# A deformable convolution and a selective scan on one core: state inputs of the last image from a block-diagonal matrix product, a moved split of the corner weighting, and ordered table loads

## The chip, the core and the metric

The kernel runs on one core of a Trainium2 chip. The core has five engines with queues of their own: TensorE (PE; its weight loads are PEld in the profile), VectorE (DVE), ScalarE (ACT), GpSimd (POOL) and SyncE (SP, which here only issues DMAs). Each engine takes its instructions strictly in the order of its queue, and waits at the head of the queue until the semaphores of that instruction are there. The metric is the time of one execution on the device in microseconds. A difference of 0.2% or less cannot be told from no change for this kernel.

## What is computed

The input is four images of 128 x 128 pixels with 128 channels, fp32. Two layers follow each other, each on a normalized copy of its input and added to it. Layer 0 is a deformable 3x3 convolution in two groups of 64 channels: an ordinary convolution gives an offset for each pixel and tap, each tap is then read at a fractional place, as a weighted sum of the four pixels around it (the "corners"), and a depthwise 3x3 and a pointwise convolution follow. Layer 1 is a two-deep stack of Mamba blocks over sequences; the kernel handles each image row of 128 pixels as a sequence of 128 steps for 256 inner channels and 16 states:

```python
out = wa[..., None]*gather(y0i, x0i) + wb[..., None]*gather(y1i, x0i) \
    + wc[..., None]*gather(y0i, x1i) + wd[..., None]*gather(y1i, x1i)
...
deltaA  = jnp.exp(jnp.einsum('btd,dn->btdn', delta, A))
deltaBu = jnp.einsum('btd,btn->btdn', delta * u, Bm)
...
def step(h, xs):
    dA, dBu, c = xs
    h = dA * h + dBu
    y = jnp.einsum('bdn,bn->bd', h, c)
    return (h, y)
```

Here `u` is a SiLU of a short convolution, `delta` a softplus of a small product, and `Bm`, `Cm` (B and C) come from the same product. The result is `(y + u * D) * silu(res)`, multiplied by an output matrix.

## The kernel before

**Stages.** Image 0's statistics and gather table come first. Then layer 0 of image 0 runs alone (`layer0`), together with the tables of the other images. Then a loop over the images lays layer 0 of image b+1 beside layer 1 of image b; for the last image only layer 1 is left. The pace is fixed in program order: for every step of the scan layer so many steps of the gather layer are issued.

**The framework orders the queues.** The kernel text gives a program order. A scheduler places the instructions in each engine's queue when the kernel is built, and may move an independent instruction forward; it keeps every dependency between tiles. `keep_in_program_order` and manual dependencies restrict it further. What it decides is fixed before the kernel runs.

**Layer 0.** Work goes in units: one of nine pairs of taps for four image rows, 288 units per image. `gather` issues eight indirect DMAs for a unit (POOL writes their descriptors), into tiles `gt` of two rows each. `sample` multiplies the gathered corners by their weights `wt` into `gw`: for the first half (h=0) as one VectorE instruction of 1024 elements (L387), for the second half (h=1) as 16 small ScalarE activations with a per-partition scale (L382). TensorE then transposes and adds the corners (L128) and multiplies by the combined convolution weights (L420).

**Layer 1.** A block is four image rows (`TB` = 512 steps); 32 blocks make an image. A job is one block and one of the two Mamba layers, 256 jobs in all; blocks go in pairs, so that the jobs run (0, layer 0), (1, layer 0), (0, layer 1), (1, layer 1). `pre` computes what a job needs: `u` (L530, L540), the gate `g` (L545, L550), the small product `dbl` (L554, L557), and `delta` and `du` = delta times u (L576 to L591). `main` runs the states, two at a time, in eight rounds q: it loads the rows of B and C broadcast over the partitions, takes the exponentials into one of three tiles `da` (L627), forms `hs` = du times B (L661), scans (L667), multiplies by C (L670), and transposes and adds into `y` in PSUM (L128). After the eighth round come the gate (L677), a transposition (L682) and the output product (L687, or L694 and L696). While `main` of a job runs, `pre` of the next one is issued one portion a round: the portion with u and g comes after round q=0.

**The last image** differs: du is turned once per job by TensorE (`turn_du`), so that time lies on the partitions and B is a per-partition scalar. POOL (L646) and ScalarE (L644) make `xs`, TensorE turns it back (L651), and VectorE scans 512 steps at a time straight from PSUM (L653), then multiplies by C (L656).

**Tables.** ScalarE holds one set of function tables at a time. Silu is in another set than Exp and Ln; where the queue changes from one to the other the compiler puts an ACT_TABLE_LOAD, which the profile shows under the line of the instruction that needed it.

Of the kernel before, what the change touches and what calls it, by code (L numbers as in the profile page):

```python
# [17 lines left out]
P = 128  # L18
G = 2
CG = 64  # L20
# [11 lines left out]
XP = DTR + 1 + 2 * NS  # L32

# [30 lines left out]
def block_kernel(ctx: ExitStack, tc: tile.TileContext, a: dict, out: bass.AP):  # L64
# [26 lines left out]
    pb = ctx.enter_context(tc.tile_pool(name="l0b", bufs=1))  # L91
    ps = ctx.enter_context(tc.tile_pool(name="l0ps", bufs=2, space=PSUM))
    psa = ctx.enter_context(tc.tile_pool(name="l0psa", bufs=2, space=PSUM))
# [11 lines left out]
    offw = loadw("offw", [P, NT, 64])  # L105
# [13 lines left out]
    wc = cw.tile([P, NT, NT, CG], F32, name="wc")  # L119
# [14 lines left out]

    dw = loadw("dw", [P, NT, NT], pool=p2, tag="dbl")
# [35 lines left out]
    xn = cw.tile([P, RB + 2, WP], F32, name="xn")  # L171
# [3 lines left out]
    sbuf_s = [cw.tile([P, 4, WP], F32, name=f"s{i}") for i in range(NSB)]  # L175
# [192 lines left out]
    def sample(b, j, u, gts):  # L368
# [3 lines left out]
        for h in range(2):  # L372
# [4 lines left out]
            if h:  # L377

                for r in range(2):
                    for s in range(4):  # L380
                        for v in range(2):
                            nc.scalar.activation(  # L382
                                gw[:, r, s, v], gts[h][:, v, r, s * CG : (s + 1) * CG], AF.Copy,
                                scale=wt[:, u, r0 + r, s, v : v + 1],
                            )
            else:
                nc.vector.tensor_tensor(  # L387
                    gw.rearrange("p r s v c -> p (r s) v c"),
                    gts[h].rearrange("p v r (s c) -> p (r s) v c", c=CG),
                    wv.unsqueeze(3).to_broadcast([P, 8, 2, CG]),  # L390
                    ALU.mult,
                )
# [100 lines left out]
    duts = []  # L493
    n_dut = [0]

    def turn_du(st, nm):

        if not duts:
            duts.append(p2.tile([P, 2, SR, NC * P], F32, tag="hs", name="duts"))
        n_dut[0] += 1  # L500
        dut = duts[0][:, n_dut[0] % 2]
# [8 lines left out]

    def pre(st, l):

        blk = st["blk"]
        nm = f"{blk}_{l}"
# [24 lines left out]
        for c in range(NC):  # L539
            nc.scalar.activation(u[:, c], pus[c], AF.Silu, bias=cvb[:, l, c : c + 1])  # L540
        g = p2.tile([P, SR, NC * P], F32, tag="g", name=f"g_{nm}", bufs=2)
        for i in range(SR // 2):
            px = ps1.tile([P, 2, NC * P], F32, tag="t", name=f"pr_{nm}_{i}")
            for j in range(2):
                nc.tensor.matmul(  # L545
                    px[:, j], h[:, 2 * i + j, DCONV - 1 :], resw[:, l, :],
                    start=(j == 0), stop=True, skip_group_check=True,
                )

            tc.keep_in_program_order(nc.scalar.activation(g[:, 2 * i : 2 * i + 2], px, AF.Silu))  # L550
# [9 lines left out]
        if in_last(blk):  # L560

            pbt = ps1.tile([P, SR, XP], F32, tag="t", name=f"pbt_{nm}")
            for i in range(SR):
                nc.tensor.transpose(pbt[:, i, :], dbl[:, i * P : (i + 1) * P], ident[0:XP, 0:XP])
# [16 lines left out]
        nc.scalar.activation(e, e, AF.Exp, scale=-1.0)  # L581
        nc.scalar.activation(w1, e, AF.Identity, bias=1.0)
        nc.scalar.activation(du, w1, AF.Ln)
        nc.scalar.activation(w1, w1, AF.Identity, bias=-1.0)
# [3 lines left out]
        nc.vector.tensor_tensor(e, w1, e, ALU.subtract)  # L588
        nc.vector.tensor_tensor(de, de, e, ALU.subtract)
        nc.vector.tensor_tensor(de, de, du, ALU.add)  # L590
        nc.vector.tensor_tensor(du, de, u, ALU.mult)  # L591
        st.update(u=u, g=g, delta=de, du=du, bcd=bcd)
        st.pop("dut", None)
        if in_last(blk) and duts:
            yield
            turn_du(st, nm)

    def main(st, l):
# [11 lines left out]
        if in_last(blk) and "dut" not in st:  # L610
            turn_du(st, nm)
        for q in range(NS // NQ):
            bc = []
            for w in range(in_last(blk), 2):
# [8 lines left out]
            for c in range(NC):  # L623
                dv = st["delta"][:, c].rearrange("p (s t) -> p s t", s=SR)
                for n in range(NQ):
                    s = q * NQ + n
                    nc.scalar.activation(  # L627
                        da[:, c, n, :, 1:], dv[:, :, 1:], AF.Exp, scale=aneg[:, l, c, s : s + 1]
                    )
            dc = da.rearrange("p c n s t -> p c (n s t)")  # L630
            cv = bc[-1].rearrange("p n t -> p (n t)").unsqueeze(1).to_broadcast([P, NC, NQ * TB])
            if in_last(blk):


                for n in range(NQ):
                    s = q * NQ + n

                    xs = (p2 if n else pb).tile(
                        [P, SR, NC * P], F32, tag="bc0" if n else "gw", name=f"xs_{nm}_{s}", bufs=2
                    )  # L640
                    for i in range(SR):
                        bv = st["bt"][:, i, s : s + 1]
                        if n:
                            nc.scalar.activation(xs[:, i], st["dut"][:, i], AF.Copy, scale=bv)  # L644
                        else:
                            nc.gpsimd.tensor_scalar(xs[:, i], st["dut"][:, i], bv, None, ALU.mult)  # L646
                    for c in range(NC):
                        pool, tag = (ps, "t") if n else (psa, "acc")
                        px = pool.tile([P, SR, P], F32, tag=tag, name=f"px_{nm}_{s}_{c}")
                        for i in range(SR):  # L650
                            nc.tensor.transpose(px[:, i, :], xs[:, i, c * P : (c + 1) * P], ident)  # L651
                        dn = da[:, c, n].rearrange("p s t -> p (s t)")
                        nc.vector.tensor_tensor_scan(  # L653
                            dn, dn, px.rearrange("p s t -> p (s t)"), 0.0, ALU.mult, ALU.add
                        )
                nc.vector.tensor_tensor(dc, dc, cv, ALU.mult)  # L656
            else:
# [165 lines left out]
```

## Time and profile before

| quantity | us |
|---|---|
| time, median of 3 runs | 25900.95 |
| lowest and highest run | 25897.37 and 25929.91 |
| span of the profiled execution, first to last instruction | 24903.2 |
| busy in the span: TensorE | 19986.7 |
| busy: VectorE | 20935.3 |
| busy: ScalarE | 16107.7 |
| busy: GpSimd | 17956.4 |

The profile is of one execution of its own, whose time from outside is not listed; its span is 997.75 us below the median of the other runs. In the profile each engine's busy time is the union of its instructions' times. Groups of instructions are listed by line, with the name of the tile written, then those read, the shapes, the count, the busy time and the mean of one in ns; after the bar stands the idle time of the engine just before them, and what ended it. L128 is the line of a helper that serves both layers, so its rows are told apart by tile names (`p` for layer 0, `y` for layer 1). A real fp32 product on TensorE shows as two records for one instruction; a transposition shows as one.

### The profile page before, as it was taken

The numbers are of one execution on the slowest core, as the hardware profiler recorded it, in microseconds if no ns is written. First come the engines' busy times: TensorE is split into PE (matmuls) and PEld (weight loads), VectorE is DVE, ScalarE is ACT, GpSimd is POOL, SyncE is SP. The second block draws the span as 40 slices with busy tenths as digits, with TensorE's granted clock in tenths as the row PEclk, the third lists the DMA queues.
The fourth block names the chain that finished last, engine by engine and source line by source line (L and its number), as shares of the span: only waits on it lengthen the run. The fifth ranks groups of instructions, "written<-read, shape, count | busy, mean of one in ns | idle before, by whom it ended". The sixth has DMA issues, their size and how long they took to land. (4 is left out here: it accounts for less than half of the span.)

```text
span 24903.2 us, 331178 instructions
## 1 busy us (share of the span) xinstructions
PE 19986.7 (80%) x121156; PEld 13946.7 (56%) x121156; DVE 20935.3 (84%) x13018; ACT 16107.7 (65%) x38037; POOL 17956.4 (72%) x11270
## 2 busy tenths in 40 slices
PE   5788788888888878888888878888888877878877
PEld 3555455555555555555555555555555556666666
DVE  2221269999999999999999999999999998888888
ACT  2444466666666666666666666666666667888887
POOL 4777777887887857788887866787887845555555
PEclk8999989999999888999999888999999889999999
DMA  4554544454444444454544444454454442222221
GB/s 136 157 159 130 151 142 157 156 161 158 158 159 156 158 145 153 157 162 157 159 161 155 159 150 151 153 163 158 159 160 157 157 138 67 69 69 71 70 69 68
DMA packets 1530815, 3471.82 MB, mean 139 GB/s; under 512 B 243283, under 2 KB 717651, under 8 KB 1529052
## 3 DMA queue, kind: packets, MB, share of 16 engines
q1 hardware_dynamic: 1086812, 2242.08, 28.0%
q0 software_dynamic: 442368, 1208.55, 15.4%
q8 instruction: 951, 15.58, 0.3%
q14 instruction: 684, 5.60, 0.1%
HBM read 3299.19 MB, written 150.47 MB: 139 GB/s over the span
## 5 line engine op out<-in xcount | busy, mean ns | idle before, releaser
L359 POOL DMA_INDIRECT gt<-table,idx x9216 | 15606.0, 1693 | 4665.8 <-issue 2582.2
L627 ACT ACTIVATE da<-de,aneg 128x508 f32<-128x508 f32 x8192 | 5455.4, 711 | 2609.2 <-PE y L128 2357.7
L667 DVE TENSOR_TENSOR_SCAN da<-da,hs 128x2048 f32<-128x2048 f32 x1536 | 6792.2, 4422 | 120.2 <-ACT da L627 23.8
L128 PE MATMUL y<-ident,da 128*128 128x128 f32 x32768 | 4753.9, 306 | 2176.1 <-DVE da L670 1901.2
L420 PE MATMUL acc<-s,wc 128*64 128x256 f32 (+3 forms) x38400 | 6060.3, 439 | 276.7 <-ACT s L401 269.1
L128 PEld LDWEIGHTS y<-ident,da 128*128 128x128 f32 x32768 | 4247.0, 159 | 2997.4 <-DVE da L670 2050.8
L382 ACT ACTIVATE gw<-gt,wt 128x64 f32<-128x64 f32 x18432 | 4613.2, 337 | 1024.2 <-DMA gt<-table,idx 592.1
L420 PEld LDWEIGHTS acc<-s,wc 128*64 128x64 f32 x38400 | 3200.8, 140 | 2440.1 <-issue 1287.5
L128 PE MATMUL p<-ident,gw 128*128 128x128 f32 x18432 | 2896.6, 305 | 1471.5 <-DVE gw L387 1215.5
L646 POOL TENSOR_SCALAR xs<-duts,bt 128x256 f32<-128x256 f32 x2048 | 2349.7, 1164 | 2249.2 <-ACT duts L508 1185.7
L661 DVE SCALAR_TENSOR_TENSOR hs<-du,ones,bc 128x1024 f32<-128x1024 f32 x3072 | 3828.0, 1281 | 0.0
L670 DVE SCALAR_TENSOR_TENSOR da<-da,ones,bc 128x2048 f32<-128x2048 f32 x1536 | 3609.6, 2350 | 31.8
L128 PEld LDWEIGHTS p<-ident,gw 128*128 128x128 f32 x18432 | 2363.9, 157 | 2272.0 <-DVE gw L387 1150.1
L387 DVE TENSOR_TENSOR gw<-gt,wt 128x1024 f32<-128x1024 f32 x1152 | 1403.7, 1219 | 2357.9 <-DMA gt<-table,idx 1883.7
L653 DVE TENSOR_TENSOR_SCAN da<-da,px 128x512 f32<-128x512 f32 x2048 | 2350.6, 1202 | 509.2 <-PE px L651 509.2
L401 ACT COPY s<-p 128x512 f32<-128x512 f32 x1152 | 669.7, 581 | 2102.5 <-PE p L128 2100.1
L530 PE MATMUL pu<-hp,inc 128*128 128x512 f32 x4096 | 1830.4, 594 | 1.1 <-ACT ot L700 0.8
L651 PE MATMUL px<-ident,xs 128*128 128x128 f32 x8192 | 1213.5, 287 | 537.8 <-DVE da L653 322.1
L651 PEld LDWEIGHTS px<-ident,xs 128*128 128x128 f32 x8192 | 972.2, 147 | 818.0 <-POOL xs L646 329.3
L530 PEld LDWEIGHTS pu<-hp,inc 128*128 128x128 f32 x4096 | 747.8, 190 | 813.1 <-issue 809.3
L656 DVE TENSOR_TENSOR da<-da,bc 128x2048 f32<-128x2048 f32 x512 | 1172.0, 2289 | 6.6
L644 ACT ACTIVATE xs<-duts,bt 128x256 f32<-128x256 f32 x2048 | 894.3, 499 | 19.3 <-PE px L651 18.8
(133 smaller groups left out, 14768.7 us busy)
## 6 DMA issues: line engine op xcount, KB each, us to landing
bc<-bcd SPq DMA_DIRECT2D x3584, 512.0 KB
gt<-table,idx POOLq DMA_INDIRECT x9216
table<-xg SPq DMA_DIRECT2D x1016, 64.0 KB
xt<-in_x SPq DMA_DIRECT2D x124, 320.0 KB
xr<-in_x SPq DMA_DIRECT2D x128, 256.0 KB
x<-xo SPq DMA_DIRECT2D x128, 256.0 KB
x1t<-x SPq DMA_DIRECT2D x128, 256.0 KB
x1t_o<-x SPq DMA_DIRECT2D x128, 256.0 KB
```

Of the source, the lines that this page charges most:

```text
L128: nc.tensor.matmul(o, v, ident, is_transpose=True, start=start, stop=stop, skip_group_check=True)
L359: nc.gpsimd.indirect_dma_start(out=gt[:, v, r], out_offset=None, in_=flat, in_offset=bass.IndirectOffsetOnAxis(ap=idx[:, ri, o : o + 1], a ...
L382: nc.scalar.activation(gw[:, r, s, v], gts[h][:, v, r, s * CG : (s + 1) * CG], AF.Copy, scale=wt[:, u, r0 + r, s, v : v + 1],)
L420: nc.tensor.matmul(accs[b, j + i0][CG * g : CG * g + CG, q : q + rb - ra, :], wc[sl, v, e, :], st[p + 4 * g if p < 4 else 8][sl, ra:rb, kx ...
L530: nc.tensor.matmul(px.rearrange("p (s t) -> p s t", s=SR), inc[:, l, j, c * P : (c + 1) * P], h[:, :, j : j + P], start=(j == 0), stop=(j ...
L627: nc.scalar.activation(da[:, c, n, :, 1:], dv[:, :, 1:], AF.Exp, scale=aneg[:, l, c, s : s + 1])
L646: nc.gpsimd.tensor_scalar(xs[:, i], st["dut"][:, i], bv, None, ALU.mult)
L651: nc.tensor.transpose(px[:, i, :], xs[:, i, c * P : (c + 1) * P], ident)
L653: nc.vector.tensor_tensor_scan(dn, dn, px.rearrange("p s t -> p (s t)"), 0.0, ALU.mult, ALU.add)
L661: nc.vector.scalar_tensor_tensor(hs[:, :, n, :], st["du"], ones[:, 0:1], bc[0][:, n].unsqueeze(1).to_broadcast([P, NC, TB]), op0=ALU.mult, ...
L667: nc.vector.tensor_tensor_scan(df, df, hs.rearrange("p c n t -> p (c n t)"), 0.0, ALU.mult, ALU.add)
L670: nc.vector.scalar_tensor_tensor(dc, dc, ones[:, 0:1], cv, op0=ALU.mult, op1=ALU.mult)
```

## The change

Four things are changed together.

1. **Last image.** Layer 0's memory is released when the last image's first `pre` gets to `du`, and four banks of PSUM and new tiles are opened in its place. delta times u of 32 time steps of each of the four rows is put beside each other, turned as before, and multiplied on TensorE by a matrix `D` that holds B on a diagonal (POOL makes it, from B and a constant mask, for four states at once). The product is written to one PSUM tile `px` for four states of one half of the channels; one scan then takes all 2048 elements. Exponentials run two rounds ahead into four tiles. `main_last` replaces the branch in `main`.
2. **Corner weighting.** For image 0 all of it goes to VectorE. For the other images ScalarE takes both rows of the second half and one of the two rows of the first half; VectorE keeps one row.
3. **Table loads.** A load of the set that holds both exp and ln is placed by hand after the Silus of each `pre`. Dependencies without a semaphore put each Exp and Ln behind the last such load, and the next Silu behind every Exp and Ln issued so far.
4. **Softplus.** The subtraction of 1 (L584 on ScalarE) is folded into the next VectorE instruction.

```diff
+    def exp(i):
+        if tables["exp"] is not None:
+            order(i, tables["exp"])
+        tables["after"].append(i)
+        return i
+
+    def silu(i):
+        if tables["after"]:
+            for j in tables["after"]:
+                order(i, j)
+            tables["after"] = []
+        elif tables["silu"] is not None:
+            order(i, tables["silu"])
+        tables["silu"] = i
+        return i
...
-            nc.scalar.activation(u[:, c], pus[c], AF.Silu, bias=cvb[:, l, c : c + 1])
+            silu(nc.scalar.activation(u[:, c], pus[c], AF.Silu, bias=cvb[:, l, c : c + 1]))
...
-            tc.keep_in_program_order(nc.scalar.activation(g[:, 2 * i : 2 * i + 2], px, AF.Silu))
+            silu(nc.scalar.activation(g[:, 2 * i : 2 * i + 2], px, AF.Silu))
+        tables["exp"] = silu(nc.scalar.preload_act_table_set("natural_log_exp_and_others"))
         yield
...
-        nc.scalar.activation(e, e, AF.Exp, scale=-1.0)
+        exp(nc.scalar.activation(e, e, AF.Exp, scale=-1.0))
         nc.scalar.activation(w1, e, AF.Identity, bias=1.0)
-        nc.scalar.activation(du, w1, AF.Ln)
-        nc.scalar.activation(w1, w1, AF.Identity, bias=-1.0)
+        exp(nc.scalar.activation(du, w1, AF.Ln))
...
-        nc.vector.tensor_tensor(e, w1, e, ALU.subtract)
+        nc.vector.scalar_tensor_tensor(e, w1, -1.0, e, op0=ALU.add, op1=ALU.subtract)
...
-                    nc.scalar.activation(
+                    exp(nc.scalar.activation(
                         da[:, c, n, :, 1:], dv[:, :, 1:], AF.Exp, scale=aneg[:, l, c, s : s + 1]
-                    )
+                    ))
...
+            alone = 2 if b == 0 else 0 if h else 1
+            for r in range(alone, 2):
+                for s in range(4):
+                    for v in range(2):
+                        nc.scalar.activation(
+                            gw[:, r, s, v], gts[h][:, v, r, s * CG : (s + 1) * CG], AF.Copy,
+                            scale=wt[:, u, r0 + r, s, v : v + 1],
+                        )
+            if alone:
                 nc.vector.tensor_tensor(
-                    gw.rearrange("p r s v c -> p (r s) v c"),
-                    gts[h].rearrange("p v r (s c) -> p (r s) v c", c=CG),
-                    wv.unsqueeze(3).to_broadcast([P, 8, 2, CG]),
+                    gw[:, 0:alone].rearrange("p r s v c -> p (r s) v c"),
+                    gts[h][:, :, 0:alone].rearrange("p v r (s c) -> p (r s) v c", c=CG),
+                    wv[:, 0 : 4 * alone].unsqueeze(3).to_broadcast([P, 4 * alone, 2, CG]),
                     ALU.mult,
                 )
...
+    def make_d(st, u):
+        d = le["r"].tile([P, SR, NU, QW], F32, tag="D", name=f"D_{st['nm']}_{u}", bufs=3)
+        nc.gpsimd.tensor_tensor(
+            d, st["bt"][:, :, NU * u : NU * u + NU].unsqueeze(3).to_broadcast([P, SR, NU, QW]),
+            mask.unsqueeze(1).unsqueeze(1).to_broadcast([P, SR, NU, QW]), ALU.mult,
+        )
+        st["D", u] = d
+
+    def fill(st, k):
+        u, c = divmod(k, NC)
+        px = le["ps"].tile([P, SR, NU, P], F32, tag="dbu", name=f"px_{st['nm']}_{k}")
+        for q in range(SR):
+            for g in range(SR):
+                o = slice(g * QW, (g + 1) * QW)
+                nc.tensor.matmul(
+                    px[:, g, :, q * QW : (q + 1) * QW],
+                    st["dut"][o, q, c * P : (c + 1) * P], st["D", u][o, q],
+                    start=True, stop=True, skip_group_check=True,
+                )
+        st["px"] = px
...
+        for k in range(nk):
+            u, c = divmod(k, NC)
+            if c == 0:
+                ct = le["r"].tile([P, NU, TB], F32, tag="ct", name=f"ct_{nm}_{u}", bufs=2)
+                n0 = NS + NU * u
+                nc.sync.dma_start(ct, st["bcd"][n0 : n0 + NU, :].partition_broadcast(P))
+                if k + NC < nk:
+                    make_d(st, u + 1)
+            if k + 2 < nk:
+                exps(st, l, k + 2)
+            elif nst:
+                exps(nst, nl, k + 2 - nk)
+            hs = le["r"].tile([P, SR, NU, P], F32, tag="he", name=f"he_{nm}_{k}", bufs=3)
+            nc.vector.tensor_tensor_scan(
+                hs.rearrange("p s n t -> p (s n t)"),
+                st.pop(("da", k)).rearrange("p s n t -> p (s n t)"),
+                st["px"].rearrange("p s n t -> p (s n t)"), 0.0, ALU.mult, ALU.add,
+            )
+            if k + 1 < nk:
+                fill(st, k + 1)
+            elif nst:
+                fill(nst, 0)
+            nc.vector.tensor_tensor(
+                hs, hs, ct.rearrange("p n (s t) -> p s n t", s=SR), ALU.mult
+            )
+            for s in range(SR):
+                for i in range(NU):
+                    add_transposed(y[:, s, c], hs[:, s, i, :], False, u == NS // NU - 1 and i == NU - 1)
+            yield
```

`exps` issues the exponentials of four states of one half; `SR` = 4 is the number of rows in a block, `QW` = 32, `NU` = 4. The four values of `g` in `fill` are four slices of 32 partitions, and each writes to a PSUM bank of its own.

## Prediction

> **What bounds the kernel now.** I read the row of slices first: it shows stages with different limits.
>
> ```profile
> DVE  2221269999999999999999999999999998888888
> ACT  2444466666666666666666666666666667888887
> POOL 4777777887887857788887866787887845555555
> ```
>
> A slice is 622.6 us. POOL leads in slices 2 to 5 (image 0's gathers alone), DVE is full from slice 7 to 33 (gathers of images 1 to 3 beside the scan layer of images 0 to 2), and falls to eight tenths at the end (the scan layer of image 3 alone). The windows put the borders at the first and last scan of L667 (columns: PE, PEld, DVE, ACT, POOL busy):
>
> ```profile
> 420.00:3340.00 2920.00, 2388.58 (x15078) 1498.61 (x15079) 655.25 (x994) 1308.02 (x4857) 2220.72 (x2223) 0.91 0.50 146
> 3340.00:20570.00 17230.00, 13968.57 (x83567) 9637.80 (x83565) 16351.24 (x8935) 11263.14 (x26734) 13273.45 (x6884) 0.90 0.48 156
> 20570.00:24903.00 4333.00, 3469.45 (x21628) 2706.43 (x21628) 3804.24 (x2876) 3468.27 (x6208) 2349.73 (x2048) 0.93 0.21 69
> ```
>
> I call them A, B, C. B has 192 jobs (one block, one layer): 17230/192 = 89.7 us each, DVE busy 16351/192 = 85.1, so 4.6 idle. C has 64 jobs: 67.5 us (L677, once a job, recurs every 67.5 us), DVE busy 59.4. Why DVE hardly rests in B is in the groups by line of 6000 to 20000 us (156 jobs):
>
> ```profile
> L667 DVE TENSOR_TENSOR_SCAN da<-da,hs 128x2048 f32<-128x2048 f32 x1248 | 5518.6, 4422 | 96.8 <-ACT da L627 20.3 <-DVE hs L661 1.0
> ...
> L387 DVE TENSOR_TENSOR gw<-gt,wt 128x1024 f32<-128x1024 f32 x708 | 860.8, 1216 | 496.6 <-DMA gt<-table,idx 464.5 <-PE p L128 27.2 <-PE y L128 4.7
> ```
>
> The scan waits on its exps for 20.3 us in all, and most DVE idle is the wait for gathers (464.5/156 = 3.0 us a job). That the exps never hold the scan is what the change touches. The timeline of one job's start shows what runs there:
>
> ```profile
> 10000.97 4.42 DVE L667 TENSOR_TENSOR_SCAN da<-da,hs 128x2048 f32<-128x2048 f32 x1
> ...
> 10006.43 2.35 DVE L670 SCALAR_TENSOR_TENSOR da<-da,ones,bc 128x2048 f32<-128x2048 f32 x1
> ...
> 10008.83 1.97 PE L128 MATMUL y<-ident,da 128*128 128x128 f32 x16 [0.61 <-DVE da L670]
> ...
> 10010.63 5.32 PE L530 MATMUL pu<-hp,inc 128*128 128x512 f32 x12
> ...
> 10011.27 4.42 DVE L667 TENSOR_TENSOR_SCAN da<-da,hs 128x2048 f32<-128x2048 f32 x1
> ...
> 10015.99 0.69 ACT L540 ACTIVATE u<-pu,w_cvb 128x512 f32<-128x512 f32 x1 [1.81 <-PE pu L530]
> ...
> 10017.90 0.60 ACT L550 ACTIVATE g<-pr 128x512 f32<-128x512 f32 x1 [0.45 <-PE pr L545]
> ```
>
> The second scan (q=1) starts at 10011.27; the last Silu of the next job ends only at 10018.50, held by PE's pu matmuls, which stand in PE's queue around the y transposes of q=0. Today nobody cares: the exps of q=1 were done before.
>
> **Part 1, the two table loads (B): the step that decides.** The new edges put the next job's Silus behind all exps issued so far, and all later exps behind the load that follows the Silus. In program order the next job's Silus come after the exps of q=0 and before those of q=1. The order of the built programs confirms it: before, 16 of a job's exps (q=0 to 3) stand ahead of the next job's last Silu at 181 of 192 borders; after the change exactly 4 do, at 191. So scan q=1 must wait for: mult of q=0 (T), y transposes, pu, Silus, load, four exps. From T, with the rows' durations:
> - y transposes 2.0; pu 16 records of 0.43 = 6.9 (the order has them wholly behind y at 138 of 182 borders looked at; elsewhere pu of the first half starts ahead): T+8.9
> - u 0.2+0.69, pr 0.1+0.86 (its PSUM buffer is freed by u), g 0.2+0.60: T+11.5 (in the trace, with half of pu_0 early: 10018.50-10008.78 = 9.7)
> - table load 1.28, four exps of 0.67, hand-over: T+15.6.
>
> DVE's own work up to scan q=1 is two hs (2.5) and often an L387: 3.5. Stall 12.1, or 8.7 where pu_0 is early: mean 11.2. From the other side, laid over the trace of before (last Silu end + 1.28 + 2.9 minus scan q=1 start, 191 borders), the mean is 15.3. I take **12.0**, near the walk, which has the new order. DVE is in order, so all behind the scan waits, then y, then the next job.
>
> Loads saved: (337+173+156)/156 = 4.3 a job to 2, 2.9 us of ACT at 1.283 each; L584 goes, 1.05. ACT is 65% busy in B, so both are worth nothing. L588 becomes a scalar_tensor_tensor, 1.22 to 1.28 (the L661 row): +0.1.
>
> **Part 2, corner weighting.** Images 1 to 3: half of each L387 moves to ACT. DVE: 1.216 to some 0.69 (L215, 128x640 at 0.824, and L220, 128x320 at 0.489, give 1.05 ns an element), 4.5 units a job: -2.4 us. ACT: 4.5 x 8 x 0.25 (2843/11328) = +9.0 us a job, to 64 of 97 us: room. The Trainium skill speaks against it: "ScalarE: Activation LUTs", Rules for kernel authors, sends mul to VectorE. The row agrees on price (sixteen ACTIVATEs 3.92 us, one L387 1.22). By the rule the move loses 9.0-2.4 = 6.6 us a job; by the rows of this stage it gains 2.4, because DVE is full and ACT is not. I take the rows.
>
> Image 0 (A): ACT's half goes to DVE, 288 more L387. A is POOL's: 2223 descriptors at 1.00+0.30. Descriptors that meet an L387 take up to 1.44 instead of 0.95; some 0.3 x 288 = +86, less POOL's waits for ACT's gw (40): **+50** (0 to 120).
>
> B: busy 85.1-2.4+0.1 = 82.8, stall 12.0, remaining idle 2.0 (of 4.6, since gathers run on in the stall; 0.5 to 4.6): 96.8 against 89.7, **+1360**.
>
> **Part 3, image 3 (C).** DVE's work hardly changes: before, four L653 and one L656 a pair of states;
>
> ```profile
> L653 DVE TENSOR_TENSOR_SCAN da<-da,px 128x512 f32<-128x512 f32 x2048 | 2350.6, 1202 | 509.2 <-PE px L651 509.2
> ...
> L656 DVE TENSOR_TENSOR da<-da,bc 128x2048 f32<-128x2048 f32 x512 | 1172.0, 2289 | 6.6
> ```
>
> after, 8 x (4.42+2.29) = 53.7, plus softplus, du in two halves and g (1.3+2.4+1.4+1.2): 60.0 a job. What can go is idle: 8.1 a job. xs on POOL (2350 us) and ACT (894), and L622, go; POOL's mask product (4 a job, 128x512, some 2 to 5 us by L646's 1.16 for 256) has 17 us each. The product itself: px has one buffer, so filling k+1 starts at the end of scan k and hides behind the mult (2.29) if it takes under 2.0. It is 16 matmuls of 128 columns; the nearest full-array row, L606 (records 0.111 apart, two a matmul), gives 16 x 0.22 to 0.25 = 3.5 to 3.95. "TensorE: Matmul & The Clock Gate", Part 3, says slices of 32 rows in different row groups run at once, 3.07 times faster for four: 1.3. The trace has only column tiles: L420's pairs start 4 ns apart, near twofold. I take 1.3. Then what is late next, from PE's new order: fill 1 has pyg, ddiag and pout of the job before inside it (ready some 12.8 after the job's first scan starts, wanted at 7.9: 4.9); fill 3 stands behind pu_1 and pr (2.1); fill 4 holds pbt, which waits behind ACT's exps (2.7). 60.0+9.7 = 69.7 against 67.5: **+140** over 64 jobs. Bounds: all hidden, 60.0, -480; fills one after another, 1.9 more on most k, 78, +670.
>
> **Sum** against the profiled span: 24903+1360+50+140 = 26453. The median is 997.75 above this span, taken as fixed (the profiled execution's own time is not given): 27450.
>
> **Rivals.**
> - *Faster: the load's wait is covered.* If Silus and exps come within what DVE still has, B falls to 82.8+2.0 = 84.8 (-940) and, with fills hidden, C to 60.0 (-480): 24530. For it: DVE is full, every part takes work off the busiest engine or off ACT. Against: one da of lead, in the order itself. It decides from a stall under 4.9 us a job; the walk finds twice that.
> - *Slower still: row groups do not overlap*, or share the weight load. C +670 in place of 140: 27980. For it: L606's row. Against: L420's tiles.
> - *Stall there, but C clears its idle* (PE finds room, fills early): C -480: 26830.
>
> **Chances.** Forecast 0.55; row groups 0.15; C cleared 0.15; faster 0.13; no change 0.02. Range: stall 10 and idle 0.5 in B (+690), C -200: 26400; the overlay's 15.3 with idle 3.0 (+2200) and C +300: 28450. I take 26300 to 28400. No change (within 0.2%, what a measurement of this kernel tells apart) needs the stall near 5. So faster 0.13, slower 0.85.
>
> **What would show it.** Right: in B a job recurs at some 97 us, DVE's slices fall to eights, and the scan's line shows idle released by ACT's exps, some 12 us a job, at q=1; the half-size weighting at 0.69; two loads a job. In C a job near 70 us, fill about 1.3 us, DVE idle released by px at k=1, 3, 4. Wrong: exps that do not hold the scan; B under 90 us a job; fills near 4 us; A moved by over 120.

## The result, and the profile after

| | before | after |
|---|---|---|
| time, median (us) | 25900.9 (25897.37 to 25929.91) | 28217.81 (28179.28 to 28228.34) |
| ratio to before | 1 | 1.0889, 95% interval 1.0874 to 1.0905 |

The change makes the kernel 2317 us slower; 27450 had been forecast, with 28400 as the upper end. The direction and the place are those of the forecast, the size is not.

To compare stage with stage, a second profile of the unchanged kernel is used. Its span is 25879.9 us, in line with the timed runs; the first one's, 24903.2, was not (more on that below). The table takes the stages (A, B and C of the prediction) from the first scan and from the gate instruction that ends each job; the time of a job is a mean without the first and last jobs of a stage.

| kernel | first stage (us) | middle, us a job | last, us a job | span | time |
|---|---|---|---|---|---|
| before, first profile | 3344 | 89.74 | 67.48 | 24903 | - |
| before, second profile | 4335 | 89.68 | 67.44 | 25880 | 25876 |
| after | 4133 | 101.77 | 71.11 | 28177 | 28218 |
| no edges | 4126 | 87.45 | 72.58 | 25552 | 25561 |
| edges only | 4325 | 102.51 | 69.68 | 28439 | 28422 |
| image 0 as before | 4296 | 101.84 | 71.10 | 28361 | 28334 |
| Silus a round later | 4065 | 91.08 | 70.89 | 26084 | 26119 |
| weighting only | 4074 | 87.70 | 67.50 | 25233 | 25277 |
| filling first | 4101 | 101.74 | 69.67 | 28048 | 27989 |
| all weighting on VectorE | 4144 | 102.35 | 71.15 | 28324 | 28328 |
| images 1 to 3 on ScalarE | 4163 | 91.46 | 67.49 | 26036 | 26022 |

Against the second profile of before the stages moved by -202, +2282 and +218 us, in sum +2298. These are the slices of the changed kernel, 704 us each:

```profile
DVE  2222237887887888888888888888888788888888
ACT  0000016666666665666666665566666664444444
POOL 3666666666666655566666664566666660000000
```

VectorE's nines have become sevens and eights all through the middle: it now rests there. POOL is lower as well, since the gathers come no faster than their buffers are emptied. The windows of the three stages (columns: PE, PEld, DVE, ACT, POOL busy, then the granted clock), changed kernel:

```profile
420.00:4130.00 3710.00, 2548.64 (x15253) 1568.90 (x15250) 985.11 (x1278) 253.30 (x464) 2349.56 (x2242) 0.82 0.40 115
4130.00:23628.00 19498.00, 14768.24 (x83633) 10042.45 (x83630) 15812.72 (x8940) 12182.99 (x33005) 12217.24 (x6887) 0.87 0.43 138
23628.00:28177.00 4549.00, 3476.12 (x29771) 2694.58 (x29770) 3770.45 (x1402) 2190.68 (x3391) 330.61 (x253) 0.82 0.18 66
```

and the kernel before, second profile:

```profile
420.00:4330.00 3910.00, 2781.83 (x15282) 1578.40 (x15283) 665.93 (x1000) 1321.47 (x4925) 2200.62 (x2245) 0.83 0.38 110
4330.00:21548.00 17218.00, 13976.27 (x83569) 9620.83 (x83567) 16350.26 (x8934) 11267.23 (x26732) 13248.43 (x6884) 0.90 0.48 156
21548.00:25879.00 4331.00, 3452.04 (x21630) 2685.95 (x21628) 3805.58 (x2877) 3468.09 (x6211) 2348.41 (x2048) 0.94 0.21 69
```

In the middle VectorE does 538 us less work (16350.26 to 15812.72) in 2280 us more time. Who keeps it waiting is in the groups by line of the middle stage, 4200 to 23600 us, changed kernel, VectorE's scan and weighting:

```profile
L699 DVE TENSOR_TENSOR_SCAN da<-da,hs 128x2048 f32<-128x2048 f32 x1527 | 6749.2, 4420 | 1864.2 <-ACT da L685 1597.4 <-issue 225.3 <-DVE hs L693 1.4
...
L390 DVE TENSOR_TENSOR gw<-gt,wt 128x512 f32<-128x512 f32 x860 | 581.3, 676 | 1666.3 <-PE p L131 827.7 <-issue 398.5 <-remote 177.5
```

and, from the same groups, POOL's gather descriptors:

```profile
L363 POOL DMA_INDIRECT gt<-table,idx x6867 | 12171.8, 1773 | 6874.5 <-ACT gw L385 4234.3 <-issue 1971.2 <-DVE gw L390 319.3
```

POOL stands 4234.3 us until ScalarE gives a gather buffer back. With 190.6 jobs in the window the scan waits 9.8 us a job, which was 0.6 before, and the weighting 8.7, which was 3.2. Two waits of about one size look like two causes. The timeline of one job's start suggests that they are one:

```profile
10045.41 2.34 DVE L702 SCALAR_TENSOR_TENSOR da<-da,ones,bc 128x2048 f32<-128x2048 f32 x1
...
10047.67 2.47 DVE L693 SCALAR_TENSOR_TENSOR hs<-du,ones,bc 128x1024 f32<-128x1024 f32 x2
10047.81 1.97 PE L131 MATMUL y<-ident,da 128*128 128x128 f32 x16 [1.66 <-DVE da L702]
10049.61 6.17 PE L568 MATMUL pu<-hp,inc 128*128 128x512 f32 x14
...
10055.62 2.07 PE L583 MATMUL pr<-w_resw,hp 128*128 128x256 f32 x8
10055.82 0.69 ACT L578 ACTIVATE u<-pu,w_cvb 128x512 f32<-128x512 f32 x1 [2.75 <-issue]
...
10057.73 0.60 ACT L588 ACTIVATE g<-pr 128x512 f32<-128x512 f32 x1 [0.45 <-issue]
10058.33 1.28 ACT L589 ACT_TABLE_LOAD   x1
10059.47 1.97 PE L131 MATMUL p<-ident,gw 128*128 128x128 f32 x16
10059.63 2.55 ACT L685 ACTIVATE da<-de,aneg 128x508 f32<-128x508 f32 x4
...
10063.15 0.69 DVE L390 TENSOR_TENSOR gw<-gt,wt 128x512 f32<-128x512 f32 x1 [13.00 <-remote]
10063.75 4.42 DVE L699 TENSOR_TENSOR_SCAN da<-da,hs 128x2048 f32<-128x2048 f32 x1
```

Read it downwards: the multiplication of q=0, the y transposes, pu, pr, the Silus, the table load, four exps, and only then the scan of q=1. VectorE has nothing to do from 10050.14 to 10063.15. Here the wait is booked on the weighting, because an L390 happens to stand ahead of the scan in VectorE's queue, and its own buffer is freed by corner transposes that stand behind pu, pr and pdb in TensorE's queue. In this job the four exps had ended at 10062.18, and L390 came last. That is not the rule: over 188 jobs the scan of q=1 starts 0.03 us after the last of its four exps in the median and 0.4 us in the mean, whether an L390 stands ahead of it (94 jobs) or not. It is the exps behind the table load that end the wait, whatever line it is booked on. So the sum of both lines, up to the scan of q=1, is the figure to follow: 17.9 us a job after the change, 12.6 with the edges alone. Counting every instruction of VectorE, it is 18.0 after, 13.5 with the edges alone and 0.5 before.

### The profile page after: what moved, and what is told of

The parts are those of the page before. It is cut to its first block, busy times and chain, and to the rows that moved or that the text cites. A ratio compares the mean times of both kernels' runs of the same rounds, so it can differ in the third digit from the quotient of the medians.

```text
span 28177.5 us, 340879 instructions
## 1 busy us (share of the span) xinstructions
PE 20933.6 (74%) x129348; PEld 14397.5 (51%) x129348; DVE 20699.0 (73%) x11838; ACT 14641.9 (52%) x36886; POOL 14990.1 (53%) x9478
## 4 chain that ended last, share of the span: by engine, by line
DVE 37%; PE 20%; issue 17%; ACT 8%; another core or an unknown queue 7%; POOL 7%; DMA 3%; SPq 0%; DVEq 0%; ACTq 0%; POOLq 0%
DVE da L699 10%; DVE da L702 8%; DVE hs L693 8%; POOL gt L363 7%; PE pu L568 4%; DVE he L768 4%; PE y L131 3%; PE acc L423 3%; DMA gt<-table,idx 2%; ACT da L685 2%; PE pr L583 2%; PE p L131 2%; DVE he L777 2%; ACT gw L385 1%
## 5 line engine op out<-in xcount | busy, mean ns | idle before, releaser
L363 POOL DMA_INDIRECT gt<-table,idx x9216 | 14650.6, 1590 | 8594.3 <-ACT gw L385 4287.0
L131 PE MATMUL y<-ident,da 128*128 128x128 f32 x24576 | 3866.1, 324 | 2555.9 <-DVE da L702 2539.3
L131 PEld LDWEIGHTS y<-ident,da 128*128 128x128 f32 x24576 | 3467.9, 170 | 3262.3 <-DVE da L702 2835.9
L685 ACT ACTIVATE da<-de,aneg 128x508 f32<-128x508 f32 x6144 | 4040.8, 713 | 1192.9 <-PE y L131 1145.5
L390 DVE TENSOR_TENSOR gw<-gt,wt 128x512 f32<-128x512 f32 (+1 forms) x1440 | 1278.1, 895 | 3141.0 <-remote 1232.7
L768 DVE TENSOR_TENSOR_SCAN he<-dae,px 128x2048 f32<-128x2048 f32 x512 | 2261.2, 4416 | 678.8 <-PE px L737 675.9
L718 ACT ACTIVATE dae<-de,aneg 128x508 f32<-128x508 f32 x2048 | 1286.2, 707 | 730.3 <-DVE de L634 631.3
L131 PE MATMUL y<-ident,he 128*128 128x128 f32 x8192 | 1366.2, 335 | 276.0 <-DVE he L777 275.2
L131 PEld LDWEIGHTS y<-ident,he 128*128 128x128 f32 x8192 | 1217.1, 176 | 374.8 <-DVE he L777 336.4
L680 ACT COPY da<-zero 128x16 f32<-128x16 f32 x1536 | 329.3, 215 | 1902.4 <-PE y L131 1182.0
L737 PE MATMUL px<-D,dut 32*128 32x128 f32 x16384 | 849.0, 327 | 617.6 <-DVE he L768 617.3
```

The costliest lines, as they stand in the source:

```text
L131: nc.tensor.matmul(o, v, ident, is_transpose=True, start=start, stop=stop, skip_group_check=True)
L363: nc.gpsimd.indirect_dma_start(out=gt[:, v, r], out_offset=None, in_=flat, in_offset=bass.IndirectOffsetOnAxis(ap=idx[:, ri, o : o + 1], a ...
L390: nc.vector.tensor_tensor(gw[:, 0:alone].rearrange("p r s v c -> p (r s) v c"), gts[h][:, :, 0:alone].rearrange("p v r (s c) -> p (r s) v ...
L685: exp(nc.scalar.activation(da[:, c, n, :, 1:], dv[:, :, 1:], AF.Exp, scale=aneg[:, l, c, s : s + 1]))
L718: exp(nc.scalar.activation(da[:, :, i, 1:], dv[:, :, 1:], AF.Exp, scale=aneg[:, l, c, n : n + 1]))
L768: nc.vector.tensor_tensor_scan(hs.rearrange("p s n t -> p (s n t)"), st.pop(("da", k)).rearrange("p s n t -> p (s n t)"), st["px"].rearran ...
```

## The experiments

### The kernel before once more

> The kernel before, unchanged, for a second profile. My sum took the 997.75 us between its profiled span (24903.2) and its median (25900.95) as a fixed amount outside the span. Theory 1 (fixed amount): a second profile has a span near 24903 again and a time near 25900. Theory 2 (the first profile was of an unusually quick execution): the span comes within 100 us of the median, so near 25850, and the 950 us stand inside it, mostly in the first stage (image 0's gathers alone, 3340 us in the first profile, then near 4100) as waits of VectorE and ScalarE for semaphores that come some 10 us late.

The time was 25876.28 us and the span 25879.9: theory 2. Middle and last stage agree with the first profile within 0.1 us a job; the whole difference of 977 us lies in the first stage (3344 to 4335). Image 0's gathers and products, the same program, took 990 us longer, at a granted clock of 0.83 in place of 0.91. TensorE's convolution product shows it; first profile, 420 to 3340 us:

```profile
L420 PE MATMUL acc<-s,wc 128*64 128x256 f32 (+7 forms) x9240 | 1461.9, 443 | 25.4 <-ACT s L401 22.9
```

and the second, 420 to 4330 us:

```profile
L420 PE MATMUL acc<-s,wc 128*64 128x256 f32 (+7 forms) x9364 | 1747.4, 462 | 516.4 <-issue 324.1 <-ACT s L401 176.8
```

Nearly the same number of instructions now has 324 us of "issue" ahead of it, pauses for which the profile shows no cause. The profiles of all other kernels have a first stage above 4060 us, as the timed runs need it, and 104 to 380 us of "issue" ahead of this product. So the first stage that the forecast was worked out on was the exception.

### Edges off, edges alone

```diff
 def exp(i):
-    if tables["exp"] is not None:
-        order(i, tables["exp"])
-    tables["after"].append(i)
     return i
...
 def silu(i):
-    if tables["after"]:
...
     return i
...
-    silu(nc.scalar.activation(g[:, 2 * i : 2 * i + 2], px, AF.Silu))
-tables["exp"] = silu(nc.scalar.preload_act_table_set("natural_log_exp_and_others"))
+    tc.keep_in_program_order(nc.scalar.activation(g[:, 2 * i : 2 * i + 2], px, AF.Silu))
```

> The changed kernel without the edges that keep Silus and exps apart, and without the table load placed by hand (the compiler places the loads again); all else as changed. Theory 1 (the edges and the load make the stall of the scan at q=1): the middle stage falls from 101.8 us a job to 88 to 92, the scan's wait for ScalarE's exps from 8.3 us a job to under 1, and the time falls by 1900 to 2600 us, to 25600 to 26300. Theory 2 (the moved corner weighting on ScalarE holds the middle stage): the scan still waits, the middle stage stays above 98 and the time falls by less than 700.

The time was 25561.09 us, ratio to before 0.9882 (0.9866 to 0.9899): faster than the kernel before. The middle stage fell to 87.45 us a job. Its groups by line, 4200 to 20900 us:

```profile
L688 DVE TENSOR_TENSOR_SCAN da<-da,hs 128x2048 f32<-128x2048 f32 x1529 | 6762.8, 4423 | 385.6 <-ACT da L674 221.6 <-issue 71.1 <-DVE hs L682 1.5
...
L390 DVE TENSOR_TENSOR gw<-gt,wt 128x512 f32<-128x512 f32 x859 | 583.0, 679 | 312.8 <-DMA gt<-table,idx 107.0 <-PE p L131 101.9 <-remote 63.7
```

Both waits go together, 1864.2 to 385.6 and 1666.3 to 312.8, as one cause demands. The wait for exps is 1.2 us a job, a little over the 1 that theory 1 allowed; time and stage came out slightly below its bands.

The other way round, the kernel before with the edges and the load placed by hand and nothing else:

> The kernel before with only the edges between Silus and exps and the load placed by hand. Theory 1: the scan of the middle stage waits for its exps for 8 to 12 us a job, the middle stage goes from 89.7 to 98 to 102 us a job (+1600 to +2300), the last stage, whose scans are fed by ScalarE as well, by 0 to 4 us a job; time 27500 to 28300. Theory 2: the edges alone cost under 500 us, and the loss needs the moved weighting.

The time was 28422.14 us, ratio 1.0983 (1.0961 to 1.1005), and the middle stage 102.51 us a job: slightly more than theory 1's upper ends. The edges alone cost more than the whole change. The two waits are there again, 4400 to 23900 us:

```profile
L695 DVE TENSOR_TENSOR_SCAN da<-da,hs 128x2048 f32<-128x2048 f32 x1523 | 6730.4, 4419 | 1466.6 <-ACT da L655 1113.9 <-issue 315.4 <-DVE hs L689 0.9
...
L387 DVE TENSOR_TENSOR gw<-gt,wt 128x1024 f32<-128x1024 f32 x859 | 1041.7, 1213 | 1656.0 <-DMA gt<-table,idx 678.5 <-PE p L128 622.6 <-remote 236.7
```

The four corners of the middle stage now stand: old share of the weighting 89.68 without and 102.51 with edges, new share 87.45 (or 87.70, weighting only) without and 101.77 with. The edges cost 12.8 to 14.3 us a job. The last stage rose by 2.2 a job.

### Image 0's weighting as before

```diff
-alone = 2 if b == 0 else 0 if h else 1
+alone = (0 if h else 2) if b == 0 else 0 if h else 1
```

> The changed kernel with image 0's corner weighting shared between VectorE and ScalarE as before the change. Theory 1 (VectorE's in-order queue, which now holds both halves, makes the first stage 4132 us long in place of 3344): the first stage returns to 3340 to 3450 and the time falls by 700 to 800, to 27400 to 27500. Theory 2 (the late semaphores of the first stage have another cause, and the kernel before has them too in most executions): the first stage stays within 100 us of 4130 and the time within 100 of 28200.

The first stage was 4296 us, so theory 1 fell. Theory 2 was right in kind, but 4296 lies 66 us outside its band, and the time, 28334.12 us, 34 us outside: the new share has an effect of its own, of the other sign than forecast. All of image 0's weighting on VectorE makes the first stage 163 us shorter (4296 to 4133). The other profiles agree: with the old share it takes 4296 to 4335 us (three profiles, the first one of before left aside), with the new one 4065 to 4163 (seven). Why is only argued: one VectorE instruction of 1.22 us replaces sixteen activations in the path from the gather to TensorE. POOL's wait for ScalarE's `gw`, 339.1 us in this experiment, is no longer among its three largest in the changed kernel.

### Silus a round later, edges kept

```diff
         for c in range(NC):
             ...
+        if not in_last(blk):
+            yield
         for c in range(NC):
             silu(...)
...
-        if not in_last(blk):
-            yield
         nc.vector.scalar_tensor_tensor(e, w1, -1.0, e, ...)
...
                 df, df, hs.rearrange("p c n t -> p (c n t)"), 0.0, ALU.mult, ALU.add
             )
+            yield
             nc.vector.scalar_tensor_tensor(dc, dc, ones[:, 0:1], cv, ...)
...
-            yield
         finish(st, l, y)
```

> The changed kernel with the edges and the hand-placed load kept, but in images 0 to 2 the next job's pu matmuls issued ahead of the y transposes of q=0, and its Silus and their load one round later, between the exps of q=1 and those of q=2. Theory 1 (the stall is the barrier standing where pu cannot yet have run, so that ScalarE, the corner weighting in its queue and the scan all wait for TensorE): the scan's and the weighting's idle time at q=0 and q=1 (17.9 us a job now) nearly goes, the middle stage falls from 101.8 to 85.5 to 89 us a job, two loads a job stay, time 25100 to 25800. Theory 2 (a barrier between Silus and exps costs its stall wherever it stands, or the load is what costs): the stall moves to q=2, the middle stage stays above 96, time above 27000.

Moving the `yield`s does two things together: the pu products are issued ahead of the y transposes of q=0, and the Silus with their load a round later. The time was 26119.07 us, ratio 1.0107 (1.009 to 1.0124). The middle stage came to 91.08 us a job: 10.7 of the 14.3 that the edges cost are won back, with the same edges and the same two loads a job. This goes against theory 2: where the barrier stands, against the products that it waits for, decides. Which of the two moves does more was not taken apart. And 91.08 us and 26119 us are outside theory 1's bands too. What is left, groups of 4200 to 21500 us:

```profile
L699 DVE TENSOR_TENSOR_SCAN da<-da,hs 128x2048 f32<-128x2048 f32 x1521 | 6725.5, 4422 | 1034.8 <-ACT da L685 615.7 <-issue 364.6 <-DVE hs L693 1.4
...
L390 DVE TENSOR_TENSOR gw<-gt,wt 128x512 f32<-128x512 f32 x855 | 578.4, 677 | 432.5 <-issue 300.4 <-PE p L131 62.8 <-ACT da L685 31.5
```

The idle time ahead of the first three scans of a job is 7.3 us by scan and weighting (17.9 before it, up to the second scan), and nearly all of it now stands at q=2, as theory 2 had it for the place. In most jobs pu does not get through TensorE in the one round that it was given: in the 143 of 188 jobs that lose over 4 us at q=2, its last record ends 3.0 us after the scan of q=1 in the median; in the other 45 it ends 1.1 us before.

### The weighting alone

The new `alone` lines in the kernel before, nothing else.

> The kernel before with only the new share of the corner weighting (all of image 0's on VectorE, three quarters of the others' on ScalarE). Theory 1 (the three parts add, and the edges are the only loss of the middle stage): the first stage 4335 to 4130, the middle stage 89.7 to about 87.4 us a job, the last unchanged at 67.4; time 25886 - 200 - 430 = 25250 (25150 to 25350). Theory 2 (the middle stage's gain without edges came from the last image's product or the cheaper softplus, not from the weighting): the middle stage stays above 89, time above 25550.

The time was 25277.47 us, ratio 0.9779 (0.9763 to 0.9796), the fastest of all kernels here. First stage -261, middle -389 (87.70 us a job), last +3: together -647, and 25880 - 647 = 25233 is the span. Theory 1 holds in every stage, with the first one 56 us shorter than it said.

Against this kernel the one without edges has the new product of the last image and the shorter softplus besides. Its middle stage is the same within 0.3 us a job, and its last stage takes 72.58 us a job in place of 67.50. Without the edges, what was done for the last image costs 5.1 us a job there.

### The whole weighting on one engine

In the changed kernel `alone = 2` everywhere:

> The changed kernel with all corner weighting of all images on VectorE, none on ScalarE; edges and last image as changed. The idle time of VectorE at q=0 and q=1 (scan and weighting together) is 12.6 us a job with half of the weighting on ScalarE (edges alone) and 17.9 with three quarters. Theory 1 (the weighting queued in ScalarE around the barrier adds to the barrier's own wait): with none of it the idle time there falls to 8 to 11, the weighting's own part of it under 2; VectorE's work rises by 7.9 to 90.4 and the middle stage lies at 99 to 102 us a job. Theory 2 (the idle time is the barrier's chain through pu and Silus alone): it stays at 12.6 or more and the middle stage goes above 103.5.

The time was 28327.77 us. The idle time at q=0 and q=1 was 11.9 us a job, and the middle stage 102.35 us a job. The idle time lies between theory 1's 8 to 11 and theory 2's 12.6, the stage between 102 and 103.5, so neither holds as written; the weighting's own part stayed at 8.5, where theory 1 wanted under 2. With none, half and three quarters of the weighting on ScalarE the idle time is 11.9, 12.6 and 17.9: most of it is the barrier's own chain, and the weighting in ScalarE's queue does not explain the wait booked on L390.

In the kernel with the weighting alone, `alone = 2 if b == 0 else 0`:

> The kernel before with all of image 0's corner weighting on VectorE and all of images 1 to 3's on ScalarE. Theory 1 (VectorE still bounds the middle stage when ScalarE has no barrier): VectorE loses the last 3.05 us of weighting a job, the middle stage falls from 87.7 to 84.5 to 86 us a job, time 24700 to 24950. Theory 2 (ScalarE, 67 of 87.7 us busy and then 76, holds exps and gathers): the middle stage stays at 87.5 or more, time at or above 25250.

The time was 26021.57 us, ratio 1.0051 (1.0034 to 1.0068), the middle stage 91.46: theory 2, and well above the lower bounds that it gave. From 4200 to 20800 us ScalarE is then 14074 of 16600 us busy (85%), VectorE 14595, and the scans wait 7.7 us a job (1394.2 us in all). Of the three shares tried without edges (half, three quarters, all on ScalarE: 89.68, 87.70, 91.46), three quarters is the best.

### The filling ahead of the job's end

```diff
-        y = psy.tile([P, SR, NC, P], F32, tag="y", name=f"y_{nm}")
+        def begin():
+            if "fin" in le:
+                finish(*le.pop("fin"))
+            y = psy.tile([P, SR, NC, P], F32, tag="y", name=f"y_{nm}")
...
+            return y
...
+            if k == 0:
+                y = begin()
             nc.vector.tensor_tensor(
                 hs, hs, ct.rearrange("p n (s t) -> p s n t", s=SR), ALU.mult
             )
...
-        finish(st, l, y)
+        if nst:
+            le["fin"] = (st, l, y)
+        else:
+            finish(st, l, y)
```

> The changed kernel with, in image 3, the end of the job before (g, pyg, pout) and the ddiag product issued after the filling of k=1 instead of ahead of it. Theory 1 (scan k=1 waits 4.7 us a job because that filling stands behind them in TensorE's queue): VectorE's idle time ahead of scan k=1 falls under 0.5, the last stage from 71.1 to 66 to 67 us a job, time 28218 - 300 = 27920. Theory 2 (the wait only moves: g comes later, and the next job's pu and fillings with it): the last stage stays above 69.5 us a job and the time within 120 of 28218.

The time was 27988.73 us. The wait at k=1 went from 4.7 us a job to nothing, as theory 1 said, but 3.8 us came up at k=2. The last stage fell from 71.11 to 69.67 us a job, 92 us over 64 jobs, and the time by 229, which is outside theory 2's 120. The kernel before was 45 us quicker in the same round too (25855.63 against 25900.9), and the two profiles differ in the other stages, so the smaller figure is the safer one. The wait mostly moves, which is theory 2. In the groups of the last stage, changed kernel, 23700 to 28100 us,

```profile
L768 DVE TENSOR_TENSOR_SCAN he<-dae,px 128x2048 f32<-128x2048 f32 x495 | 2186.1, 4416 | 660.9 <-PE px L737 658.0 <-ACT e L626 2.7
```

and in this experiment, 23700 to 28000 us,

```profile
L775 DVE TENSOR_TENSOR_SCAN he<-dae,px 128x2048 f32<-128x2048 f32 x494 | 2181.9, 4417 | 569.7 <-PE px L737 569.6
```

the idle time released by px falls by 88 us only.

## Why the prediction was right, and where it was not

**Why it was slower: right.** The edges and the hand-placed load are the loss, shown from both sides. The signs named in advance are there: VectorE's slices down from nine tenths, mostly to eight, the scan's wait for exps at q=1, the half-size weighting at 0.676 us (0.69 forecast), and two loads a job, 4200 to 23600 us:

```profile
L578 ACT ACT_TABLE_LOAD x191 | 245.1, 1283 | 3.3
L589 ACT ACT_TABLE_LOAD x191 | 245.1, 1283 | 1.0
```

**The middle stage: one term of three mis-sized.** A job was forecast at 96.8 us and took 101.77.

| term, us a job | forecast | measured |
|---|---|---|
| VectorE busy | 82.8 | 82.4 |
| stall at the barrier | 12.0 | 18.0 |
| other idle | 2.0 | 1.4 |

The step that failed is "I take 12.0, near the walk, which has the new order". The walk itself was good for the case it walked. From the end of the multiplication (T) it put the end of pu at T+8.9, the Silus at T+11.5 and the scan at T+15.6. With the edges alone these are T+8.4, T+11.1 and T+15.5 in the mean of the 154 jobs (of 188) that have this order. In the changed kernel 102 of 188 jobs have it, at T+9.6, T+12.1 and T+16.2 in the median. Three things were missing. They are worked out here over the same 188 jobs.

The first is small. In the changed kernel VectorE has 2.5 us of work of its own between the multiplication and the scan, not the 3.5 of the walk, because L390 stands behind the wait. Where the order is that of the walk and nothing comes late (73 jobs) the scan is at T+16.3 and the stall 13.9 us.

The second is the order. In the other 86 jobs the end of the job before stands between the multiplication and pu; one of them, job start at 15004.85:

```profile
15004.85 1.22 DVE L791 TENSOR_TENSOR g<-y,g 128x1024 f32<-128x1024 f32 x1
...
15006.12 1.78 PE L796 MATMUL pyg<-ident,g 128*128 128x128 f32 x8 [3.50 <-DVE g L791]
...
15011.82 1.50 PE L666 MATMUL y<-ddiag,u 128*128 128x128 f32 x12
...
15014.91 7.03 PE L568 MATMUL pu<-hp,inc 128*128 128x512 f32 x16
...
15030.11 0.69 ACT L578 ACTIVATE u<-pu,w_cvb 128x512 f32<-128x512 f32 x1 [4.98 <-remote]
...
15037.91 0.69 DVE L390 TENSOR_TENSOR gw<-gt,wt 128x512 f32<-128x512 f32 x1 [28.85 <-PE p L131]
```

Here g comes after the first scan. The product with ddiag needs the `y` that g has just read, and the y transposes of q=0 wait behind it, so that pu starts 8.8 us after g's end; in the median of these jobs it ends at T+13.0 and the scan follows at T+20.1. The walk had the y transposes start at T. But VectorE's work of the job's end fills part of this: in the 60 of these jobs in which nothing comes late the stall is 15.3 us.

The third is the largest, and no walk over the records shows it: TensorE's results come late. In 55 of the 188 jobs, of both orders, ScalarE begins a Silu u more than 1 us after the last pu record that it reads has ended, 7.7 us in the median (0.04 in the other 133). It stands idle meanwhile, at u or at a small copy ahead of it (L680), and both wait for TensorE. In the job above these records end at 15018.50 and 15021.94, and the two u start at 15024.44 and 15030.11. The stall of these 55 jobs is 26.7 us, against 14.5 in the other 133; together they make the 18.0. So of the 6.0 us that were missed the late jobs are 3.5. With the edges alone only 13 jobs of 188 are late, with all weighting on VectorE 11: that is most of the way from 12.6 to 17.9. TensorE's granted clock over the wait is 0.84 in the late jobs and 0.98 in the others. Whether it makes the results late or falls because TensorE stands is not shown; in the job above it had been 1.0 from 15009.78 to 15026.84.

The overlay on the trace of before gave 15.3 and was set aside for the walk; the truth lay above both, and a walk of one job is no mean over jobs.

**The first stage: wrong in sign.** Forecast +50, measured -202, of which 163 are image 0's share; the rest, 39 us, is no more than profiles differ (4065 to 4163 with this share). A move of over 120 us had been named as a sign of being wrong. The forecast costed POOL's descriptors, 2222.5 us of the 2920 in the first profile. In the second profile they are 2200.62 of 3910 us, so in the executions that the times come from POOL waits more; that the shorter path through VectorE then counts is likely, and not shown.

**The fixed amount.** The 997.75 us between span and median were taken as lying outside the span. They lie inside, in the first stage. The sum was not hurt by it only because the changed kernel has them as well, and that was luck.

**The last stage: right place by place, a little short.** Forecast 4.9, 2.1 and 2.7 us of waiting at k=1, 3 and 4; measured 4.7, 2.0 and 3.0. Not foreseen were 1.2 us ahead of softplus' first VectorE instruction and 0.8 at k=7; VectorE's work was 58.9 us (3770.45 over 64 jobs) in place of 60.0; hence 71.1 in place of 69.7. What the edges do here was not costed by itself. Alone they make the old last stage 2.2 us a job longer (67.44 to 69.68), with the new product 1.5 shorter (72.58 to 71.11); why is open. The row groups do run together: this is the job start at 25041 us,

```profile
25041.19 0.93 PE L737 MATMUL px<-D,dut 32*128 32x128 f32 x12 [2.36 <-DVE he L768]
...
25042.31 1.97 PE L796 MATMUL pyg<-ident,g 128*128 128x128 f32 x8 [0.18 <-DVE g L791]
...
25049.06 0.94 PE L737 MATMUL px<-D,dut 32*128 32x128 f32 x20
25050.11 4.42 DVE L768 TENSOR_TENSOR_SCAN he<-dae,px 128x2048 f32<-128x2048 f32 x1 [5.66 <-PE px L737]
...
25055.26 1.17 PE L737 MATMUL px<-D,dut 32*128 32x128 f32 x32
```

A filling of one piece, 32 records, takes 1.17 us at a granted clock of 1.0 (229 of the 512 fillings; 1.3 forecast, 3.5 to 3.95 if the groups ran in turn), and up to 2.1 us at a lower one. In one such piece the four groups' records start 3 to 7 ns apart. One reading behind the forecast does not hold: the pairs of L420 in the trace of before do not start 4 ns apart, but mostly 6 to 14 or 50 to 60 ns; the forecast of 1.3 does not rest on it alone. The filling of k=1 is cut in two, with pyg and the job's end between: the wait named in advance. The last stage is not made faster by a product this cheap: px has one buffer, and VectorE waits for its filling. A second buffer was not tried.

**The rule against the row.** For the moved half of the weighting the Trainium skill ("ScalarE: Activation LUTs", Rules for kernel authors), which sends `mul` to VectorE, would by the prediction's estimate have made the job 6.6 us longer, the rows 2.4 shorter. Alone the move makes it 2.0 shorter (89.68 to 87.70). The row was right, as ScalarE had room in this stage: with three quarters of the weighting it was 77% busy. With the last quarter moved too, the job is 3.8 us longer than that, and the rule has its say.

**The rivals.** The faster one fell with the stall: 18 us where it needed under 5. Row groups one after another fell with the 1.17 us of a filling. A last stage that clears its idle time fell with the 10 us of waiting for px.

**The sum.** 922 us too little in the middle (2282 against 1360), 252 too much in the first stage, 78 too little in the last; with 20 us between spans and medians, the 768 us from 27450 to 28218. That the time stayed under 28400 owes something to luck: the middle stage (101.77) came out above what the upper end allowed for it (82.8 + 15.3 + 3.0 = 101.1), and with the first stage as forecast the time would have been 28470.

**What stays open.** Why TensorE's results come late in some jobs is not known. Why the wait on L390 remains at 8.5 us a job when ScalarE does no weighting is only argued (corner transposes behind pu, pr and pdb in TensorE's queue). A deeper `gw` would test it; it was not tried. It can give little by itself: the scan of q=1 starts 1.8 us after its exps there in the mean, and 0.4 in the changed kernel.

## What to carry to other kernels

An edge that groups instructions by function table saves loads of 1.28 us on an engine with room, and costs whatever the group's latest input costs: place it where those inputs are already there, or leave the engine its loads. When costing such a barrier, walk it for every order that the queues show and weigh the cases by how often they occur, and allow for late results that no walk shows; one job's walk gave 12 us, the two orders weighed without late jobs 14.5, and the mean was 18. And when a profile's span and the timed runs differ by 4%, profile again before costing any stage.

## What the runs showed of the hardware

TensorE has times in which it runs slower than its records explain. In the first profile of the kernel before, one unit's convolution product took 7.33 us from 348.31 (56 records), at a granted clock of 1.0. In the second the same product, begun at 373.21, was still running at 392.7, some 19 us, with pauses of about 0.6 us and more ahead of single weight loads where they had been 0.19. These pauses have begun by 378.3, while the clock is recorded at 1.0; it falls to 0.5 at 383.3, and its mean over 373 to 392 us is 0.86. The copies of ScalarE and VectorE's next weighting wait behind it. Over the first stage this product has 286 us more busy time and 491 us more idle time ahead of it than in the first profile, 777 of the 990 us by which the stage is longer. Such pauses are in every profile but the first one, and late results are seen in 55 of 188 jobs of the middle stage with the whole change. Around that stretch no instruction fetch fits it: a packet of 16 KB every 20 to 40 us, about 1 us each, as in the first profile. The cause was not found.
